# A spectral-convolution kernel: the forward transform along x folded a second time

## The chip, the cores and the metric

The kernel runs on one core of a Trainium2 chip. It is one program with one launch, all in 32-bit floats. The metric is the device time of one execution in microseconds, from the first to the last instruction and what lies around it. The kernel before takes 3254.34 us, the median of three runs (3249.64 to 3259.84).

The core has five instruction queues: TensorE (matrix products, PE in the profile, with its weight loads listed as PEld), VectorE (DVE), ScalarE (ACT), GpSimd (POOL) and SyncE (SP, which here only starts transfers). Each queue is worked off in order; queues wait for each other through semaphores. SBUF is the on-chip memory of 128 partitions, PSUM the small memory into which TensorE writes.

## The reference

The input x has 16 batches, 16 channels and 256 x 256 points. Two layers follow each other, each adding its output to its input.

```python
x = x + L0(group_norm(x))          # a circular 3x3 convolution, 16 -> 16 channels
x = x + L1(group_norm(x))          # a "Laplace" layer:
    alpha = fft2(v)                                        # v: the normalised map
    A, Bm = 1/(i*omega1 - pole1), 1/(i*omega2 - pole2)
    S  = einsum('ikpq,oikp,xikq->oxik', residue, A, Bm)
    x1 = ifft2(einsum('biox,oxik->bkox', alpha, S)).real
    x2 = a few modes: alpha summed against A and Bm, times exponentials in y and x
    return x1 + x2 / 65536
```

So the second layer takes a two-dimensional Fourier transform of 256 maps of 256 x 256, mixes the channels for each pair of frequencies with weights that depend on the frequency, and transforms back. What is changed here is the first of these steps, the forward transform.

## The kernel before, in words

The program has four stages, one after the other.

**Convolution (from 0 to about 764 us).** The convolution of layer 0 is run on TensorE, its output v is written to the scratch tensor `vD` in memory, and the tables that the later stages need are made on the side: `make_hat` fills `tabE`, `tabO` and `hB` from the constants `hatT`, `make_exps` the exponentials. The order of this stage is written out by hand (`manual_schedule`): the loop over `g` issues the convolution's products and advances the table generators by a step now and then.

**Forward transform (about 773 to 1513 us): the stage that is changed.** Its loop runs over the 16 channels `i`, and within each over four groups of four batches `b0`; one such step, of which there are 64, is called a block here. A block has three parts.

- `fold` (lines 583 to 600) loads four maps, `vy`, with the upper and the lower half of y side by side. Since a cosine or sine table of 256 points is symmetric or antisymmetric, the sum and difference of mirrored points can be taken first, and half a table is then enough. GpSimd takes sum and difference of the two halves of y (`s`, lines 590 and 591, 128 x 1024 each). VectorE then folds x in the same way, adding and subtracting the mirrored columns of `s` (`vf`, lines 595, 598 and 599); line 595 also subtracts the mean.
- `lines` (lines 602 to 630) transforms along y: for each of the four maps and each of the two x-parities, one product with `vf` as weights against `tabE` and one against `tabO`, into `ps_y`. Each product of 32-bit floats is two instructions in the profile. ScalarE copies the result to `t` and scales it (line 624).
- `columns` transforms along x: a small product for the few modes of x2 (`psd`, line 637), and for each pair of maps two products of 128 x 128 tables, `sinF` and `cosF`, against 512 columns of `t` (`ps_x`, line 648), one per x-parity. ScalarE copies the odd part to `q` (line 651), VectorE builds the four combinations of even and odd in `spec` (lines 654 to 657), ScalarE and GpSimd set two special frequencies (lines 660 and 661).

After the four blocks of a channel `spec` is written to the scratch tensor `aD` (line 675, started from ScalarE's queue), and `psd` is multiplied with coefficients and summed into `acc` (line 687 on VectorE, line 688 on GpSimd, twice a channel).

The order within this stage isn't written out. The framework's scheduler sets each engine's order from the order of the program, what depends on what, and the number of buffers: three of `vy`, two of `s`, two of `vf`, two of `t`, three PSUM banks for `ps_x`, two of `spec`, one of `pr`.

**Mixing (to about 2440 us)** and **inverse transform (to the end)** follow; in the mixing stage the order is again written by hand. They read `aD` in the order in which the forward transform left the frequencies, and tables (`inv`, `kgrp`) that fit that order. The inverse stage (lines 985 to 1001) ends with sums on VectorE, lines 995 to 1001, beside GpSimd's line 960; these lines are looked at below because they show the two engines at work together.

Of the kernel before, what the change touches and what calls it, by code (L numbers as in the profile page):

```python
# [9 lines left out]
FP = mybir.dt.float32  # L10
AF = mybir.ActivationFunctionType
ALU = mybir.AluOpType
# [5 lines left out]
C = 16  # L18
N = 256
P = 128  # L20
# [4 lines left out]
def conv_then_laplace_kernel(ctx: ExitStack, tc: tile.TileContext, a: dict, out: bass.AP):  # L25
# [15 lines left out]
    nc = tc.nc  # L41
    x = a["x"]
# [4 lines left out]
    def const(name, shape, src=None):  # L47
        t = cp.tile(shape, FP, name=name, tag=name)
        nc.sync.dma_start(out=t, in_=a[name] if src is None else src)
        return t  # L50

    cols = const("cols", [P, 24])
    kmask = const("kmask", [P, C])
    trig = const("trig", [P, 2, P])
    o2 = cp.tile([P, B, 2, 64], FP, name="o2", tag="o2")

    vD = [dp.tile([2, P, C, N], FP, name=f"vD{b}", tag=f"vD{b}") for b in range(B)]
# [22 lines left out]
    tabE = tp.tile([P, C + 1, P], FP, name="tabE", tag="tabE")  # L80
    tabO = tp.tile([P, C + 1, P], FP, name="tabO", tag="tabO")
    hB = tp.tile([P, 2, C, P], FP, name="hB", tag="hB")
    coef = [tp.tile([P, C, 4, 4, 2], FP, name=f"coef{j}", tag=f"coef{j}") for j in range(2)]
    nc.vector.tensor_copy(tabE[:, 0], trig[:, 0])
    nc.vector.tensor_copy(tabO[:, C], trig[:, 1])

# [4 lines left out]
    p1 = ExitStack()  # L93
    wp = p1.enter_context(tc.tile_pool(name="conv_w", bufs=1))
    xp = p1.enter_context(tc.tile_pool(name="xt", bufs=5))
    vp = p1.enter_context(tc.tile_pool(name="vt", bufs=5))
    sp = p1.enter_context(tc.tile_pool(name="stats", bufs=2))
# [14 lines left out]
    def load1(name, shape):  # L112
        t = wp.tile(shape, FP, name=name, tag=name)
        nc.sync.dma_start(out=t, in_=a[name])
        return t
# [2 lines left out]
    imask = load1("imask", [P, 2, 3, 32])  # L118
    g128 = load1("g128", [P, P])
    m16 = load1("m16", [P, C])  # L120
    hatT = load1("hatT", [P, 2, 3, 2, P])
    ones = wp.tile([P, P], FP, name="ones", tag="ones")
    nc.vector.memset(ones, 1.0)

# [184 lines left out]
    def make_hat(side):  # L309


        kcol = sw.tile([P, 2], FP, name="s_kcol", tag="s_kcol")
        nc.sync.dma_start(out=kcol, in_=a["kcol"])
        omega(kcol, kcol, rd[:, side : side + 1])
        n = C * C * 4
        to = ((tabE[:, 1:], tabO[:, :C]), (hB[:, 0], hB[:, 1]))[side]
        for half in range(2):
            pb = sw.tile([P, n // 2, 2], FP, name="s_pb", tag="s_pb")
            nc.sync.dma_start(
                out=pb,  # L320
                in_=a[f"pole{side + 1}"][half * 512 : half * 512 + 512].partition_broadcast(P),
            )
            yield
            re = [sw.tile([P, n // 2], FP, name="s_re", tag=f"s_re{h}") for h in range(2)]
            im = [sw.tile([P, n // 2], FP, name="s_im", tag=f"s_im{h}") for h in range(2)]
            dens = [sw.tile([P, n // 2], FP, name="s_den", tag=f"s_den{h}") for h in range(2)]
            pr, pi = pb[:, :, 0], pb[:, :, 1]
            for h in range(2):
                k = kcol[:, h : h + 1]
                nc.scalar.activation(im[h], pi, AF.Identity, bias=k, scale=-1.0)  # L330
                nc.scalar.activation(dens[h], pi, AF.Square, bias=k, scale=-1.0)
                if h == 0:
                    nc.gpsimd.tensor_tensor(re[1], pr, pr, ALU.mult)
                nc.gpsimd.tensor_tensor(dens[h], dens[h], re[1], ALU.add)
                yield
            for h in range(2):
                w, r, den = im[h], re[h], dens[h]
                nc.vector.reciprocal(den, den)
                yield

                nc.gpsimd.tensor_tensor(r, pr, den, ALU.mult)
                nc.vector.scalar_tensor_tensor(w, w, -1.0, den, ALU.mult, ALU.mult)
                yield
            yield
            for eo in range(2):
                hv = to[eo].rearrange("p i (m r) -> p i m r", r=2)[:, 8 * half : 8 * half + 8]
                for ri in range(2):
                    ps = psu.tile([P, 512], FP, name="ps_setup", tag="ps_setup")
                    for h in range(2):

                        parts = (((2, re), (1, im)), ((0, im), (1, re)))[ri]
                        for j, (at, src) in enumerate(parts):
                            nc.tensor.matmul(
                                ps,
                                lhsT=hatT[:, h, at, eo],
                                rhs=src[h],
                                start=h == 0 and j == 0,
                                stop=h == 1 and j == 1,
                            )
                        yield  # L360
                    nc.scalar.copy(hv[:, :, :, ri], ps.rearrange("p (i m) -> p i m", i=8))
# [173 lines left out]
    for g in range(24 * B + 3):  # L535
        conv(g)
        b, n = divmod(g, 24)
# [22 lines left out]
    p1 = ExitStack()  # L560
    kp = p1.enter_context(tc.tile_pool(name="b_const", bufs=1))
    vp = p1.enter_context(tc.tile_pool(name="vy", bufs=3))
    sp = p1.enter_context(tc.tile_pool(name="fold_y", bufs=2))
    fp = p1.enter_context(tc.tile_pool(name="fold_x", bufs=2))
    lp = p1.enter_context(tc.tile_pool(name="lines", bufs=2))
    kpp = p1.enter_context(tc.tile_pool(name="sines", bufs=3))
# [9 lines left out]
    nc.vector.memset(sgn[:, 0:1], -1.0)  # L576
    nc.vector.memset(sgn[:, 1:2], 1.0)
    acc = kp.tile([P, 2, B, 16, 2], FP, name="acc", tag="acc")
    cosF, sinF = trig[:, 0], trig[:, 1]
    m, n = cols[:, 16:17], cols[:, 17:18]  # L580

    def fold(i, b0):

        vy = vp.tile([P, 2, 4, N], FP, name="vy", tag="vy")
        for j in range(4):
            nc.sync.dma_start(
                out=vy[:, :, j], in_=vD[b0 + j][:, :, i, :].rearrange("h y x -> y h x")
            )
        s = sp.tile([P, 2, 4, N], FP, name="s", tag="s")
        nc.gpsimd.tensor_tensor(s[:, 0], vy[:, 0], vy[:, 1], ALU.add)  # L590
        nc.gpsimd.tensor_tensor(s[:, 1], vy[:, 0], vy[:, 1], ALU.subtract)
        vf = fp.tile([P, 2, 2, 4, P], FP, name="vf", tag="vf")
        lo, hi = s[:, :, :, 0:P], s[:, :, :, N - 1 : P - 1 : -1]
        for j in range(4):
            nc.vector.scalar_tensor_tensor(  # L595
                vf[:, 0, 0, j], lo[:, 0, j], vmr[:, 1, b0 + j, i : i + 1], hi[:, 0, j], ALU.add, ALU.add
            )
        nc.vector.tensor_tensor(vf[:, 0, 1], lo[:, 1], hi[:, 1], ALU.add)  # L598
        nc.vector.tensor_tensor(vf[:, 1], lo, hi, ALU.subtract)
        return vf  # L600

    def lines(i, b0, vf):

# [28 lines left out]
    def columns(i, b0, t, spec, psd):  # L632

        for kq in range(4):
            rows = slice(32 * kq, 32 * kq + 32)
            for xo in range(2):
                nc.tensor.matmul(
                    psd[rows, b0 : b0 + 4],
                    lhsT=hB[:, xo, i, rows],
                    rhs=t[:, xo, :, 1, rows],  # L640
                    start=xo == 0,
                    stop=xo == 1,
                )
        for j in range(0, 4, 2):
            bs = slice(b0 + j, b0 + j + 2)
            ps = [px.tile([P, 2, 2, P], FP, name="ps_x", tag="ps_x") for _ in range(2)]
            for xo, tab in ((1, sinF), (0, cosF)):
                nc.tensor.matmul(ps[xo], lhsT=tab, rhs=t[:, xo, j : j + 2, 0:3:2], start=True, stop=True)  # L648
            even, odd = (z.rearrange("p b t f -> p t f b") for z in ps)
            q = kpp.tile([P, 2, P, 2], FP, name="q", tag="q")  # L650
            nc.scalar.copy(q, odd)
            lo, hi = slice(0, P), slice(P, N)
            st = nc.vector.scalar_tensor_tensor
            st(spec[:, 0, lo, bs], q[:, 1], m, even[:, 0], ALU.mult, ALU.add)
            st(spec[:, 1, lo, bs], q[:, 0], m, even[:, 1], ALU.mult, ALU.subtract)
            st(spec[:, 0, hi, bs], even[:, 0], n, q[:, 1], ALU.mult, ALU.add)
            st(spec[:, 1, hi, bs], even[:, 1], n, q[:, 0], ALU.mult, ALU.subtract)

            flat = spec.rearrange("p r f b -> p (r f) b")
            nc.scalar.copy(flat[:, 0:385:384, bs], even[:, :, 0])  # L660
            nc.gpsimd.tensor_tensor(
                flat[:, 256:127:-128, bs],
                q[:, :, 0],
                sgn.unsqueeze(2).to_broadcast([P, 2, 2]),
                ALU.mult,
            )
# [342 lines left out]
def _constants():  # L1009
# [7 lines left out]
    tcos = np.cos(np.pi * (np.outer(half, p) % (2 * N)) / N)  # L1017
    tsin = np.sin(np.pi * (np.outer(half, f_sin) % (2 * N)) / N)
    c["trig"] = np.stack([tcos, tsin], 1)
    w = 2.0 / N**2  # L1020
    c["inv"] = np.stack([w * tcos.T, w * tsin.T, -w * tsin.T, tcos.T, tsin.T], 1)

    th = 2 * np.pi * (np.outer(j, j) % N) / N
    t = np.stack([np.cos(th), np.sin(th)]).reshape(2, 2, P, N)
    t = np.stack([t[..., :P] + t[..., : P - 1 : -1], t[..., :P] - t[..., : P - 1 : -1]], 3) / 2

    c["hatT"] = np.concatenate([t, -t[:1]]).transpose(2, 1, 0, 3, 4)
    k = (j + P) % N - P
    c["kcol"] = k.reshape(2, P).T
    c["kslot"] = np.concatenate([p, -f_sin])[None]  # L1030
# [14 lines left out]
    cols[:, 20:24] = p[:, None] // 32 == np.arange(4)  # L1045
    c["cols"] = cols

    fx = np.arange(P).reshape(32, 4)
    fx = np.concatenate([fx, [[P, 1, 2, 3]]])
    st = p // 32 % 2  # L1050
    c["kgrp"] = np.where((fx == P) & (st == 0)[:, None, None], -fx, fx)
    mcol = np.zeros((P, 9))
# [89 lines left out]
```

## Time and profile before

| | |
|---|---|
| median of the runs | 3254.34 us |
| the profiled execution | 3263.39 us, span 3261.5 us |
| TensorE busy | 2731.3 us (84% of the span) |
| VectorE busy | 1840.4 us (56%) |
| ScalarE busy | 1342.9 us (41%) |
| GpSimd busy | 942.9 us (29%) |
| mean granted TensorE clock | 0.939 of full speed |
| memory traffic | 193 GB/s over the span |

The profile describes one execution, which took 0.3% more than the median. Its page gives the engines' shares, the queues, the chain of work that ended last and the costliest groups of instructions; the trace behind it can be asked for any stretch: the order of the instructions (the timeline), the busy time by stretch, the duration of every instruction of a line, and who waited for whom. "L595" is line 595 of the kernel before. "128x512" is a tile of 128 partitions with 512 elements in each. In the timeline, consecutive instructions of one line are merged into one entry, with their number behind the x.

### The profile page before, as it was taken

The numbers are of one execution on the slowest core, as the hardware profiler recorded it, in microseconds if no ns is written. First come the engines' busy times: TensorE is split into PE (matmuls) and PEld (weight loads), VectorE is DVE, ScalarE is ACT, GpSimd is POOL, SyncE is SP. The second block draws the span as 40 slices with busy tenths as digits, with TensorE's granted clock in tenths as the row PEclk, the third lists the DMA queues.
The fourth block names the chain that finished last, engine by engine and source line by source line (L and its number), as shares of the span: only waits on it lengthen the run. The fifth ranks groups of instructions, "written<-read, shape, count | busy, mean of one in ns | idle before, by whom it ended". The sixth has DMA issues, their size and how long they took to land.

```text
span 3261.5 us, 104676 instructions
## 1 busy us (share of the span) xinstructions
PE 2731.3 (84%) x46188; PEld 1949.9 (60%) x46188; DVE 1840.4 (56%) x3584; ACT 1342.9 (41%) x2640; POOL 942.9 (29%) x753
## 2 busy tenths in 40 slices
PE   4878787796999999996676777777749999999998
PEld 1333333344777677764444545555438998999987
DVE  5555665565555555555343333334317888788787
ACT  2454676563444444442233333333313333333333
POOL 1111111002444455442111111111105444444442
PEclk9899898898999999997799899999979999999999
DMA  5455565665445555444265555655576776767764
GB/s 215 162 187 172 200 237 195 222 222 171 173 164 203 198 194 185 167 165 182 81 175 160 158 160 163 173 163 168 166 242 231 259 259 235 281 239 252 267 223 155
DMA packets 409158, 637.89 MB, mean 196 GB/s; under 512 B 30336, under 2 KB 364544, under 8 KB 400128
## 3 DMA queue, kind: packets, MB, share of 16 engines
q1 hardware_dynamic: 338816, 496.96, 46.8%
q10 hardware_dynamic: 69888, 134.23, 10.8%
q8 instruction: 364, 5.96, 0.7%
q14 instruction: 90, 0.74, 0.1%
HBM read 353.72 MB, written 277.35 MB: 193 GB/s over the span
## 4 chain that ended last, share of the span: by engine, by line
PE 47%; issue 10%; DVE 4%; DMA 4%; POOL 1%; ACT 1%; ACTq 0%; SPq 0%; DVEq 0%; POOLq 0%
PE ps_s L791 10%; PE ps_mix L839 9%; PE ps_f L990 5%; PE ps_f L991 5%; PE ps_p L985 5%; PE ps_x L648 3%; PE ps_y L608 3%; PE ps_y L616 3%; DMA out_y<-ol 3%; PE ps_h L974 2%; DVE ol L998 1%; DVE ol L1001 1%; DVE ol L997 1%; DVE sg L902 1%; DMA vl<-vD 1%
## 5 line engine op out<-in xcount | busy, mean ns | idle before, releaser
L223 PE MATMUL ps_conv<-xt,wc 32*32 32x512 f32 x12288 | 485.6, 646 | 29.9 <-ACT vt L241 20.8
L960 POOL TENSOR_TENSOR u<-yk 128x512 f32<-128x512 f32 x256 | 340.1, 1357 | 487.9 <-PE ps_p L985 411.3
L791 PE MATMUL ps_s<-ct,w 64*32 64x256 f32 (+1 forms) x8448 | 326.9, 415 | 132.6 <-issue 69.4
L839 PE MATMUL ps_mix<-abd,sg 128*32 128x64 f32 x16384 | 297.7, 229 | 134.9 <-issue 134.5
L839 PEld LDWEIGHTS ps_mix<-abd,sg 128*32 128x32 f32 x16384 | 262.8, 116 | 209.6 <-issue 199.1
L223 PEld LDWEIGHTS ps_conv<-xt,wc 32*32 32x32 f32 x12288 | 230.9, 107 | 235.9 <-issue 144.2
L902 DVE COPY sg<-ps_s 128x512 f32<-128x512 f32 x248 | 172.4, 699 | 342.8 <-PE ps_s L791 342.7
L624 ACT ACTIVATE t<-ps_y,vmr 128x768 f32<-128x768 f32 x256 | 229.7, 900 | 261.0 <-PE ps_y L616 235.9
L767 POOL TENSOR_TENSOR w<-v,mcol 128x2048 f32<-128x2048 f32 x33 | 118.8, 3599 | 717.2 <-DVE v L764 694.1
L608 PE MATMUL ps_y<-tabE,vf 128*128 128x256 f32 x1024 | 308.5, 383 | 17.1 <-DVE vf L595 13.2
L902 ACT COPY sg<-ps_s 128x512 f32<-128x512 f32 x248 | 168.5, 681 | 371.7 <-PE ps_s L791 371.6
L990 PE MATMUL ps_f<-pt,inv 128*128 128x256 f32 x1024 | 318.7, 393 | 0.3
L985 PEld LDWEIGHTS ps_p<-inv,u 128*128 128x128 f32 x2048 | 289.5, 192 | 33.7 <-POOL u L963 14.2
L616 PE MATMUL ps_y<-tabO,vf 128*128 128x256 f32 x1024 | 306.0, 381 | 2.0 <-DVE vf L598 2.0
L791 PEld LDWEIGHTS ps_s<-ct,w 64*32 64x32 f32 x8448 | 163.6, 115 | 239.4 <-issue 113.4
L991 PE MATMUL ps_f<-hs,et 128*128 128x256 f32 x1024 | 305.0, 379 | 0.0
L985 PE MATMUL ps_p<-inv,u 128*128 128x128 f32 x2048 | 291.2, 275 | 13.5 <-POOL u L963 13.5
L993 ACT COPY q<-ps_f 128x256 f32<-128x256 f32 x256 | 95.3, 372 | 432.7 <-PE ps_f L991 388.8
L590 POOL TENSOR_TENSOR s<-vy 128x1024 f32<-128x1024 f32 x64 | 151.7, 2371 | 419.9 <-issue 289.3
L648 PE MATMUL ps_x<-t,trig 128*128 128x512 f32 x512 | 247.3, 605 | 0.0
L253 DVE BATCH_NORM_STATS2 vst<-vt 128x6 f32<-128x512 f32 x128 | 88.0, 687 | 278.1 <-ACT vt L241 278.1
L608 PEld LDWEIGHTS ps_y<-tabE,vf 128*128 128x128 f32 x1024 | 193.9, 191 | 78.9 <-issue 43.8
(197 smaller groups left out, 4162.4 us busy)
## 6 DMA issues: line engine op xcount, KB each, us to landing
xt<-in_x SPq DMA_DIRECT2D x32, 2193.0 KB, 9.4
vD<-vt SPq DMA_DIRECT2D x256, 256.0 KB, 3.1
vy<-vD SPq DMA_DIRECT2D x256, 256.0 KB, 4.2
aD<-spec ACTq DMA_DIRECT2D x16, 4096.0 KB, 14.0
abd<-aD SPq DMA_DIRECT2D x512, 128.0 KB, 3.1
yD<-yt SPq DMA_DIRECT2D x256, 256.0 KB, 4.5
yk<-yD SPq DMA_DIRECT2D x16, 4096.0 KB, 14.2
vl<-vD SPq DMA_DIRECT2D x256, 256.0 KB, 6.3
```

Source lines behind the costliest of these rows:

```text
L223: nc.tensor.matmul(acc[r][32 * c : 32 * c + 32], lhsT=ready[b][0][rows, phase, tap], rhs=halves[b][u // 2][rows, q : q + 5 : 4, 2 - tap : ...
L608: nc.tensor.matmul(ps[:, xo, 0:N], lhsT=vf[:, xo, 0, j], rhs=tabE[:, 0 : i + 2 : i + 1], start=True, stop=False, skip_group_check=True,)
L616: nc.tensor.matmul(ps[:, xo, P : P + N], lhsT=vf[:, xo, 1, j], rhs=tabO[:, i : C + 1 : C - i], start=False, stop=True, skip_group_check=True,)
L624: nc.scalar.activation(t[:, :, j].rearrange("p e l n -> p e (l n)"), ps[:, :, 0:384], AF.Copy, scale=vmr[:, 0, b0 + j, i : i + 1],)
L648: nc.tensor.matmul(ps[xo], lhsT=tab, rhs=t[:, xo, j : j + 2, 0:3:2], start=True, stop=True)
L791: nc.tensor.matmul(ps[odd][32 * iq : 32 * iq + 32, ro, fy], lhsT=w[rows, iq, kk, ro], rhs=ct[rows, iq, kk, fy], start=True, stop=True,)
L839: nc.tensor.matmul(ps[32 * c : 32 * c + 32, j], lhsT=sg[:, 64 * c + 8 * n + j], rhs=abd[n // 2][:, :, c, 8 * (n % 2) + j], start=True, sto ...
L902: (nc.scalar.copy, nc.vector.tensor_copy)[j % 2](o, src)
L960: nc.gpsimd.tensor_tensor(u[:, :, j].rearrange("p b (c n) -> p c b n", c=4), in0, in1, o)
L985: nc.tensor.matmul(ps[:, at], lhsT=u[:, j, n], rhs=tab, start=True, stop=True)
L990: nc.tensor.matmul(ps[:, e], lhsT=tab, rhs=pt[:, e], start=True, stop=False)
L991: nc.tensor.matmul(ps[:, e], lhsT=et[:, 0, k, e], rhs=hs, start=False, stop=True)
```

## The change

The columns of `vf` are folded once more. After the first fold, `vf` holds 128 columns for the even and 128 for the odd x-parity. The change adds and subtracts the mirrored halves of these 128 columns into a new tile `vq`, for the one parity on VectorE and for the other on GpSimd. The products along y take `vq` as weights in place of `vf`, with the same shapes. The transform along x then needs only 64 x 64 tables: in place of two products with 128 x 128 tables for each pair of maps there are four with 64 x 64 tables (`fold2`), each on its own quarter of the TensorE array, with rows 0 to 63 or 64 to 127 of `t` as input and partitions 0 to 63 or 64 to 127 of `ps[xo]` as output.

The frequencies then come out in the order even, odd. The tables that are tied to this order (`inv`, `kgrp`) are permuted on the host; their sizes and uses stay. The x2 table `hB` has to be folded in the same way, so that `hatT` exists in two forms, one for each axis, and is loaded at the beginning of each of the two `make_hat` calls instead of once at the start. The table `trig` is no longer kept in SBUF: its two halves are loaded straight to `tabE[:, 0]` and `tabO[:, C]`, where VectorE copied them before.

The buffers change too: `s` has one instead of two, `vf` one instead of two, and the new `vq` two.

```diff
-    trig = const("trig", [P, 2, P])
...
-    nc.vector.tensor_copy(tabE[:, 0], trig[:, 0])
-    nc.vector.tensor_copy(tabO[:, C], trig[:, 1])
+    nc.sync.dma_start(out=tabE[:, 0], in_=a["trig"][:, 0])
+    nc.sync.dma_start(out=tabO[:, C], in_=a["trig"][:, 1])
...
-    hatT = load1("hatT", [P, 2, 3, 2, P])
...
     def make_hat(side):
+        hatT = wp.tile([P, 2, 3, 2, P], FP, name="hatT", tag="hatT")
+        nc.sync.dma_start(out=hatT, in_=a[f"hatT{side}"])
...
-    sp = p1.enter_context(tc.tile_pool(name="fold_y", bufs=2))
+    sp = p1.enter_context(tc.tile_pool(name="fold_y", bufs=1))
+    f1 = p1.enter_context(tc.tile_pool(name="fold_1", bufs=1))
     fp = p1.enter_context(tc.tile_pool(name="fold_x", bufs=2))
...
-    cosF, sinF = trig[:, 0], trig[:, 1]
+    fold2 = kp.tile([P, 2, 64], FP, name="fold2", tag="fold2")
+    nc.sync.dma_start(out=fold2, in_=a["fold2"])
...
-        vf = fp.tile([P, 2, 2, 4, P], FP, name="vf", tag="vf")
+        vf = f1.tile([P, 2, 2, 4, P], FP, name="vf", tag="vf")
...
-        return vf
+        vq = fp.tile([P, 2, 2, 4, 2, 64], FP, name="vq", tag="vq")
+        for xo, eng in ((0, nc.vector), (1, nc.gpsimd)):
+            lo, hi = vf[:, xo, :, :, 0:64], vf[:, xo, :, :, P - 1 : 63 : -1]
+            eng.tensor_tensor(vq[:, xo, :, :, 0], lo, hi, ALU.add)
+            eng.tensor_tensor(vq[:, xo, :, :, 1], lo, hi, ALU.subtract)
+        return vq.rearrange("p e o b h x -> p e o b (h x)")
...
-            for xo, tab in ((1, sinF), (0, cosF)):
-                nc.tensor.matmul(ps[xo], lhsT=tab, rhs=t[:, xo, j : j + 2, 0:3:2], start=True, stop=True)
+            for h in range(2):
+                rows = slice(64 * h, 64 * h + 64)
+                for xo in range(2):
+                    to = 64 * (h ^ xo)
+                    nc.tensor.matmul(
+                        ps[xo][to : to + 64],
+                        lhsT=fold2[rows, xo],
+                        rhs=t[rows, xo, j : j + 2, 0:3:2],
+                        start=True,
+                        stop=True,
+                    )
...
-    fx = np.arange(P).reshape(32, 4)
-    fx = np.concatenate([fx, [[P, 1, 2, 3]]])
+    fx = o.reshape(32, 4)
+    fx = np.concatenate([fx, [[P, *fx[0, 1:]]]])
```

More of the change, by code (lines that the diff above doesn't have):

```diff
@@ L1019, in _constants @@
     c["trig"] = np.stack([tcos, tsin], 1)
+    o = p.reshape(64, 2).T.ravel()
+    c["fold2"] = np.stack(
+        [
+            np.concatenate([tcos[:64, 0::2], tcos[:64, 1::2]]),
+            np.concatenate([tsin[:64, 1::2], tsin[:64, 0::2]]),
+        ],
+        1,
+    )
     w = 2.0 / N**2
-    c["inv"] = np.stack([w * tcos.T, w * tsin.T, -w * tsin.T, tcos.T, tsin.T], 1)
+    c["inv"] = np.stack([w * tcos.T[o], w * tsin.T[o], -w * tsin.T[o], tcos.T, tsin.T], 1)
     th = 2 * np.pi * (np.outer(j, j) % N) / N
@@ L1025, in _constants @@
     t = np.stack([t[..., :P] + t[..., : P - 1 : -1], t[..., :P] - t[..., : P - 1 : -1]], 3) / 2
-    c["hatT"] = np.concatenate([t, -t[:1]]).transpose(2, 1, 0, 3, 4)
+    t = np.concatenate([t, -t[:1]]).transpose(2, 1, 0, 3, 4)
+    c["hatT0"] = t
+    lo, hi = t[..., :64], t[..., :63:-1]
+    c["hatT1"] = np.concatenate([lo + hi, lo - hi], -1) / 2
     k = (j + P) % N - P
```

## The prediction, made before the result was known

> **What bounds the kernel now.** The change lives in the forward transform, so I first asked for busy times by stretch, then for who waited there, then for the timeline of one block.
>
> The busy times of the stretch from 855 to 1480 us (columns: length; busy us and instructions of PE, PEld, DVE, ACT, POOL; clock, DMA share, GB/s):
>
> ```profile
> 855.00:1480.00 625.00, 622.82 (x3117) 438.19 (x3117) 353.45 (x809) 275.39 (x444) 309.79 (x249) 1.00 0.51 183
> ```
>
> TensorE is busy in 622.82 of 625 us at full clock: it is the bound, and nothing else is near. In the view of waits for 800 to 1480 us, VectorE waits for TensorE (total us, times, longest):
>
> ```profile
> DVE vf L595 <- PE ps_y L616: 255.7, 61, 5.2
> ```
>
> A channel (four blocks) takes 44.93 us in the chain of waits (its start recurs at 1056.64, 1101.55, 1146.49, 1191.44 us), so a block takes 11.23 us. The timeline of one block:
>
> ```profile
> 1306.83 1.88 PE L648 MATMUL ps_x<-t,trig 128*128 128x512 f32 x4
> 1307.03 1.14 DVE L595 SCALAR_TENSOR_TENSOR vf<-s,vmr 128x128 f32<-128x128 f32 x4 [5.12 <-PE ps_y L616]
> 1308.09 0.68 DVE L598 TENSOR_TENSOR vf<-s 128x512 f32<-128x512 f32 x1
> 1308.64 0.66 PE L637 MATMUL psd<-t,hB 128*32 128x128 f32 x16
> 1308.69 1.21 DVE L599 TENSOR_TENSOR vf<-s 128x1024 f32<-128x1024 f32 x1
> 1309.83 0.47 DVE L654 SCALAR_TENSOR_TENSOR spec<-q,cols,ps_x 128x256 f32<-128x256 f32 x1
> 1310.04 2.37 POOL L590 TENSOR_TENSOR s<-vy 128x1024 f32<-128x1024 f32 x1 [6.13 <-issue]
> 1312.37 2.35 POOL L591 TENSOR_TENSOR s<-vy 128x1024 f32<-128x1024 f32 x1
> 1314.69 0.34 POOL L661 TENSOR_TENSOR spec<-q,sgn 128x4 f32<-128x4 f32 x2
> ```
>
> The reader is to see that GpSimd starts `s` 0.2 us after VectorE ends `vf` (its buffer becomes free), so the two never work on SBUF together here. Where they do, it shows at the start of the stage:
>
> ```profile
> 782.51 2.34 POOL L591 TENSOR_TENSOR s<-vy 128x1024 f32<-128x1024 f32 x1
> 782.58 7.37 DVE L595 SCALAR_TENSOR_TENSOR vf<-s,vmr 128x128 f32<-128x128 f32 x4 [3.81 <-POOL s L590]
> 784.80 2.39 POOL L590 TENSOR_TENSOR s<-vy 128x1024 f32<-128x1024 f32 x1
> 787.16 2.39 POOL L591 TENSOR_TENSOR s<-vy 128x1024 f32<-128x1024 f32 x1
> 789.88 0.68 DVE L598 TENSOR_TENSOR vf<-s 128x512 f32<-128x512 f32 x1
> ```
>
> Four VectorE instructions that take 1.14 us elsewhere take 7.37 us, until GpSimd has finished; one gets through at each of its boundaries. The inverse stage says the same of tensor_tensor: L998's row reads "409/419/1500" ns (min, median, max), the long ones beside GpSimd's L960. `spec` (one input in PSUM) keeps its 0.47 us beside GpSimd.
>
> **What the Trainium skill says.** "SBUF — State Buffer", section "Who interferes with whom": a VectorE instruction with two SBUF inputs contends with a GpSimd instruction that reads SBUF, by an exclusive lock held for the whole instruction; with at most one SBUF input it doesn't (outside two-port modes). The trace agrees: 7.37 against 1.14 us, and 0.47 us undisturbed. "TensorEngine Tiling (Array Packing)", "Key Properties": 64x64 gives four tiles that run in parallel, and a change of tiling mode drains TensorE. The trace agrees for smaller tiles: around 1902.87 us, 32 products of 64x256 on 64*32 tiles (L791) take 1.09 us, 0.034 each, where a 256-column product alone takes 0.216. The same page, "Gotcha 1: PSUM Pressure": different row tiles can't use one PSUM bank at once. The change does that (both row halves write `ps[xo]`); no row of the kernel before shows it.
>
> **The change part by part.**
>
> *TensorE.* In the chain of waits two y-products take 0.43 us and four of `ps_x` 1.72. So now: y-products 32 x 0.216 = 6.90 us, `ps_x` 8 x 0.43 = 3.44, `psd` 0.59, gaps and changes of shape 0.20: 11.13. The y-products keep shape and number. The x-products become 16 instructions of 512 columns, eight a pair of maps. Four at a time, a pair takes 2 x 0.43 = 0.86 us; two at a time (the bank rule) 1.72, as now; one at a time 3.44. I take 0.86 plus 0.2 for a drain (the second group now takes 1.91 against 1.72 after `psd`): 2 x 1.06 = 2.1, so a block of about 9.8 us. Bounds: 9.4, 11.3, 14.7.
>
> *VectorE and GpSimd.* Every piece of folding reads two SBUF tiles, so all of it shares one lock, also with GpSimd's other reads. Per block, start to start from the timeline:
>
> - `s` on GpSimd, L590 to L661's start (1310.04 to 1314.69): 4.65
> - L661, two: 0.34
> - L688, 1.27 each, two a channel: 0.63
> - `vf` on VectorE (1307.03 to 1309.83): 2.80
> - sum now: 8.42 of 11.23, so it hides under TensorE
> - added on VectorE: two of 128x512 with two SBUF inputs, like L598, 0.60 start to start: 1.20
> - added on GpSimd: two of 128x512, like L688 (1.27) and L960 (median 1.32): 2.60
> - sum after: 12.22
>
> That is more than TensorE's 9.8 and than today's 11.23. It can't be hidden: the cover (TensorE's time) is gone. The buffers serialise it too: with one `s`, GpSimd can't begin the next `s` before L599 is done; with one `vf`, VectorE can't begin the next before both halves of `vq` are made. The chain s, vf, vq, s is a circle of the same pieces. To the sum I add the channel's end, where L687 waits for L688 (0.80 us now, once in four blocks: 0.20) and hand-overs (0.14 from L599 to L590 now): 12.55 us a block. `spec` (8 x 0.39 = 3.1 us of VectorE, one SBUF input) runs beside GpSimd's 7.3 us of `s` and `vq`; if it stood in the circle, it would add up to 3.1.
>
> Bounds on the block: a VectorE instruction that slips in at a boundary costs GpSimd less than its length (2.34 becomes 2.39 above), which could save some 0.3: 11.9. All of `spec` exposed: 15.7.
>
> *The stage.* The first `s` still ends at 784.85 us. `vf` then needs 2.80, since with one `s` GpSimd no longer runs ahead, and `vq` 3.8: first y-products at about 791.4. The last block ends 63 blocks and its own products (6.9 + 0.6 + 2.1 + 0.3) later: 801.3 + 63 L, with L the block. Now the last x-product ends at 1513.2, so the difference is 63 L - 711.9. For L = 12.55: +79 us. It is zero at L = 11.30.
>
> *The rest.* `fold2` is one more transfer on SP ahead of the `vy` loads (the `jmat` issue took 0.35 us): +0.35. Loading `trig` directly takes away two VectorE copies of 0.23 us at 3.9 us, hidden by the input loads: 0. The second `hatT` load waits on SP for the last product of the first `make_hat`, with stores of `vt` and loads of `xt` behind it. That product is issued two steps of the convolution earlier (the loop has 24 x 16 + 3 = 387 in 760 us, 2 us each), so the wait is 0 to 4 us; `vt` and `xt` have five buffers, and the table is needed eight generator steps (16 convolution steps, some 31 us) later: 0. Permuted tables: 0. The later stages keep their work.
>
> Sum on the profiled execution: 3263.4 + 79 = 3342; on the median, 0.3% lower: 3254 + 79 = 3333 us.
>
> **The rivals.**
>
> *Faster: the lock doesn't set the pace.* If VectorE and GpSimd fold side by side, each alone is below TensorE (VectorE 2.8 + 1.2 + 3.1 + 0.3 = 7.4, GpSimd 4.65 + 0.97 + 2.6 = 8.2), L is 9.8, and 63 x 9.8 - 711.9 = -94: 3160 us. It decides once the shared sum drops below 11.30. For it: no steady block of the kernel before shows the collision. Against: the 7.37 us. Chance 0.08.
>
> *No change: the lock doesn't bind and the tiles don't pack.* Two row halves in one bank leave `ps_x` at 1.72 a pair, L = 11.2 to 11.3, 3250 us. Chance 0.04.
>
> *Slower still: the order wastes the lock.* VectorE is in order; if `spec` stands ahead of `vf` or waits for its PSUM banks, GpSimd waits with it and the lock lies idle. L from 13.3 to 15.7: +126 to +277, 3380 to 3531 us, 3430 in the middle. The same time would come from tiles that run one at a time (L = 14.7). For it: the order is the scheduler's, and L687 already stalls VectorE by 2.7 us a channel. Against: `spec` has 7.3 us of GpSimd work to hide in. Chance 0.23.
>
> *Forecast: the lock's sum, L from 11.9 to 13.3*, +38 to +126. Chance 0.65.
>
> **How the numbers follow.** Predicted 3333, the likeliest. The forecast alone spans 3292 to 3380. For eight in ten the range is 3290 to 3430: the forecast (0.65) and somewhat over half of the slower rival (0.15). Faster or slower than 0.3% (10 us) is about what a measurement can tell from no change: faster 0.08, within 0.04, slower 0.88.
>
> **What would show it.** The stretch's TensorE share falls from 99.7% to about 78%; a channel takes about 50 us instead of 44.93; the y-products wait for `vq`, `vf` waits for GpSimd; L595, L598 or the new VectorE lines have durations far over their 0.35, 0.68 and 0.68 us; GpSimd and VectorE's two-input work add up to nearly the whole block. `ps_x` in timelines: eight in about 1.1 us if the tiles pack, about 1.8 if the bank rule holds. The prediction is wrong if VectorE's two-input lines keep their durations beside GpSimd and TensorE stays at 99%.

## The result, and the profile after

The changed kernel takes 3487.2 us (median; 3480.1 to 3491.7), against 3252.3 us for the kernel before on the same chip: a ratio of 1.072 (1.069 to 1.074), 235 us slower. That is far over the forecast of 3333 us and over the range's upper end of 3430 us. It lies inside the rival "slower still: the order wastes the lock" (3380 to 3531 us). The profiled execution took 3484.5 us, with a span of 3482.7 us.

The last x-product of the forward transform starts at 1742.7 us now and started at 1512.6 us before, so it comes 230 us later. The spans of the two profiled executions differ by 221 us. So the whole loss is in this stage, and the later stages give a little back.

In the changed kernel the lines are shifted: `s` is L594 and L595, `vf` is L599, L602 and L603, `vq` is L608 (sum) and L609 (difference), `t` is L634, `psd` L647, `ps_x` L662, `q` L671, `spec` L674 to L677, its two special frequencies L680 (ScalarE) and L681 (GpSimd), the store of `aD` L695, `pr` L707 and `acc` L708.

The busy times of the stretch from 855 to 1480 us, columns as before (busy us and instructions of PE, PEld, DVE, ACT, POOL; clock, DMA share, GB/s):

```profile
855.00:1480.00 625.00, 494.43 (x2668) 336.15 (x2661) 398.27 (x694) 205.99 (x335) 385.75 (x272) 0.87 0.40 145
```

TensorE's share falls from 99.7% to 79%. That this is so near the 78% that were foreseen is chance: those belonged to a block of 12.55 us, the block is longer than that, and TensorE's work fills 79% of it only because a part of it ran at half clock (the mean granted clock of the stretch is 0.87, where it was 1.00; more on this at the end). Nothing takes TensorE's place: VectorE is busy for 64% of the stretch, GpSimd for 62%. So they take turns, in a circle. The view of waits from 850 to 1650 us (total us, times, longest) says who stands in it:

```profile
ACT spec L680 <- DVE spec L677: 300.1, 106, 8.4
POOL spec L681 <- DVE spec L676: 236.6, 106, 3.1
...
DVE vq L608 <- PE ps_y L626: 166.0, 53, 5.1
...
DVE vf L599 <- POOL vq L609: 108.3, 53, 4.7
...
POOL s L594 <- DVE vf L603: 55.2, 41, 2.5
```

`vf` waits for `vq` and `s` waits for `vf`: that is the circle of buffers that the prediction named. But GpSimd's largest wait is another one: for `spec`. ScalarE's largest wait is for `spec` too: its copy L680 stands in its queue ahead of `t`. The timelines of GpSimd and of VectorE in one block show why (start, length, instruction, and in brackets the idle time before it and what ended it). First GpSimd:

```profile
1311.73 2.34 POOL L594 TENSOR_TENSOR s<-vy 128x1024 f32<-128x1024 f32 x1 [1.31 <-DVE vf L603]
1314.03 2.35 POOL L595 TENSOR_TENSOR s<-vy 128x1024 f32<-128x1024 f32 x1
1316.35 1.71 POOL L608 TENSOR_TENSOR vq<-vf 128x512 f32<-128x512 f32 x1
1318.02 1.71 POOL L609 TENSOR_TENSOR vq<-vf 128x512 f32<-128x512 f32 x1
1322.83 0.20 POOL L681 TENSOR_TENSOR spec<-q,sgn 128x4 f32<-128x4 f32 x1 [3.10 <-DVE spec L676]
...
1325.91 2.35 POOL L594 TENSOR_TENSOR s<-vy 128x1024 f32<-128x1024 f32 x1 [1.31 <-DVE vf L603]
```

Then VectorE:

```profile
1315.39 1.54 DVE L608 TENSOR_TENSOR vq<-vf 128x512 f32<-128x512 f32 x1 [3.80 <-PE ps_y L626]
1316.86 1.75 DVE L609 TENSOR_TENSOR vq<-vf 128x512 f32<-128x512 f32 x1
1319.77 1.14 DVE L599 SCALAR_TENSOR_TENSOR vf<-s,vmr 128x128 f32<-128x128 f32 x4 [1.16 <-POOL vq L609]
1320.82 0.68 DVE L602 TENSOR_TENSOR vf<-s 128x512 f32<-128x512 f32 x1
1321.42 0.48 DVE L674 SCALAR_TENSOR_TENSOR spec<-q,cols,ps_x 128x256 f32<-128x256 f32 x1
...
1324.17 0.48 DVE L677 SCALAR_TENSOR_TENSOR spec<-ps_x,cols,q 128x256 f32<-128x256 f32 x1
1324.56 1.22 DVE L603 TENSOR_TENSOR vf<-s 128x1024 f32<-128x1024 f32 x1
```

The scheduler has put all eight instructions of `spec` between the second and the last part of `vf`. The next `s` needs the last part, so GpSimd stands still meanwhile. The block in order: `s` 4.62 us (1311.73 to 1316.35), `vq` on GpSimd 3.38, hand-over 0.04, the first two parts of `vf` 1.65, `spec` 3.14, L603 1.22, hand-over 0.13: 14.18 us from one `s` to the next. Over a channel it is about 59.5 us, or 14.88 a block, because the channel's end is longer (once in four blocks `pr`, `acc` and the store of `aD` come in). The prediction's own formula gives 63 x 14.88 - 711.9 = +226 us for that; measured were +235.

Two other expectations are read off here. The lock is seen at VectorE's `vq`, which waits for GpSimd (1.54 and 1.75 us in place of 0.68). And the x-products do pack: eight of them, row halves sharing a PSUM bank, take 1.09 us, where four products of 128 x 128 took 1.88:

```profile
1315.29 1.09 PE L662 MATMUL ps_x<-t,fold 64*64 64x512 f32 x8
```

### The profile page after: what moved, and what is told of

It is laid out like the page before. It is cut to its first block, busy times and chain, and to the rows that moved or that the text cites. A ratio compares the mean times of both kernels' runs of the same rounds, so it can differ in the third digit from the quotient of the medians.

```text
span 3482.7 us, 105920 instructions
## 1 busy us (share of the span) xinstructions
PE 2742.6 (79%) x46700; PEld 1943.3 (56%) x46700; DVE 2030.6 (58%) x3710; ACT 1342.1 (39%) x2640; POOL 1174.9 (34%) x881
## 4 chain that ended last, share of the span: by engine, by line
PE 35%; DVE 14%; POOL 14%; issue 8%; DMA 4%; ACT 0%; SPq 0%; ACTq 0%; POOLq 0%; DVEq 0%
PE ps_s L811 9%; PE ps_mix L859 8%; PE ps_f L1010 5%; PE ps_f L1011 4%; PE ps_p L1005 4%; POOL s L595 4%; POOL s L594 4%; DMA out_y<-ol 3%; POOL vq L608 3%; POOL vq L609 3%; PE ps_h L994 2%; DVE vf L599 2%; DVE vf L603 2%; DVE spec L675 1%; DVE spec L676 1%
## 5 line engine op out<-in xcount | busy, mean ns | idle before, releaser
L618 PE MATMUL ps_y<-tabE,vq 128*128 128x256 f32 x1024 | 375.5, 453 | 220.9 <-ACT t L634 204.9
L811 PE MATMUL ps_s<-ct,w 64*32 64x256 f32 (+1 forms) x8448 | 314.5, 402 | 133.4 <-issue 69.8
L618 PEld LDWEIGHTS ps_y<-tabE,vq 128*128 128x128 f32 x1024 | 220.1, 226 | 332.7 <-ACT t L634 229.9
L626 PE MATMUL ps_y<-tabO,vq 128*128 128x256 f32 x1024 | 354.3, 432 | 0.0
L634 ACT ACTIVATE t<-ps_y,vmr 128x768 f32<-128x768 f32 x256 | 231.4, 904 | 204.9 <-PE ps_y L626 198.1
L626 PEld LDWEIGHTS ps_y<-tabO,vq 128*128 128x128 f32 x1024 | 227.6, 222 | 41.7
L239 ACT ACTIVATE vt<-ps_conv,xq 128x512 f32<-128x512 f32 x256 | 161.3, 681 | 177.7 <-PE ps_conv L221 177.4
```

The lines of the kernel that those rows point to most:

```text
L239: nc.scalar.activation(vt if r < 2 else vt[:, ::-1], acc[r], AF.Identity, bias=ready[b][1], **by_sums)
L618: nc.tensor.matmul(ps[:, xo, 0:N], lhsT=vf[:, xo, 0, j], rhs=tabE[:, 0 : i + 2 : i + 1], start=True, stop=False, skip_group_check=True,)
L626: nc.tensor.matmul(ps[:, xo, P : P + N], lhsT=vf[:, xo, 1, j], rhs=tabO[:, i : C + 1 : C - i], start=False, stop=True, skip_group_check=True,)
L634: nc.scalar.activation(t[:, :, j].rearrange("p e l n -> p e (l n)"), ps[:, :, 0:384], AF.Copy, scale=vmr[:, 0, b0 + j, i : i + 1],)
L811: nc.tensor.matmul(ps[odd][32 * iq : 32 * iq + 32, ro, fy], lhsT=w[rows, iq, kk, ro], rhs=ct[rows, iq, kk, fy], start=True, stop=True,)
```

## The experiments

They were made in three groups, each beside the kernel before on its own chip: 3269.1 us for the first four, 3272.6 for the next four, 3256.2 for the last four. Differences are against that.

**1. `spec` behind the folds.** The folds of the next block (all lines of `vf` and `vq`) go ahead of `spec` in VectorE's order. No instruction, buffer or engine changes.

```diff
+        with tc.high_priority():
             lo, hi = s[:, :, :, 0:P], s[:, :, :, N - 1 : P - 1 : -1]
...
```

> The changed kernel with the folding on VectorE (lines of vf and vq) given precedence over spec in each engine's order, so that the two groups of spec no longer stand between the parts of vf; nothing else differs. A block of the changed kernel takes 14.88 us, of which spec takes 3.14 between two parts of vf while GpSimd waits. Theory A (the circle s, vf, vq, s on the shared lock, with spec standing in it): the block falls by about 3.0 to 11.9 us, so 63 x 11.9 - 711.9 = +38 on before, about 3292 us. Rival B (the lock's whole sum, 12.55 us, as forecast): 3333 us. Rival C (the tiled products or TensorE's clock hold the stage up): no change, about 3487 us.

Measured: 3392.6 us, +123 (ratio 1.039, 1.036 to 1.042). So the order alone gives back 111 of the 235 us. That is theory A's direction, but its +38 is missed by far. An ordinary block takes 11.39 us now in place of 14.18 (GpSimd starts `s` at 1201.32, 1212.71 and 1224.10 us). It isn't the forecast's time yet, because the channel's end has become longer: the next two `s` start at 1238.71 and 1253.67 us. ScalarE stands at the store of `aD` there for 2.27 us, with `t` behind it, and a little later for 8.45 us at its copy L681, which waits for `spec`. Its timeline:

```profile
1229.56 1.69 ACT L635 ACTIVATE t<-ps_y,vmr 128x768 f32<-128x768 f32 x2 [2.27 <-POOL spec L682]
...
1240.18 0.16 ACT L681 COPY spec<-ps_x 128x4 f32<-128x4 f32 x1 [8.45 <-DVE spec L678]
```

The copy's wait for `spec` as such isn't new: from 850 to 1650 us it adds up to 275.7 us here and to 300.1 us in the changed kernel. Experiment 6 takes the store away.

**2. The second fold alone.** The folds of the changed kernel stay, and the x-products go back to four of 128 x 128 (a table of blocks, zero elsewhere).

```diff
-            for h in range(2):
...
+            for xo in (1, 0):
+                nc.tensor.matmul(
+                    ps[xo], lhsT=fold2[:, xo], rhs=t[:, xo, j : j + 2, 0:3:2], start=True, stop=True
+                )
```

> The changed kernel with its second fold, its buffers and its order of frequencies, but the x-products as before: two products a pair with 128 x 128 tables, whose quarters are the 64 x 64 tables or zero. TensorE's block is back at about 11.1 us. Theory A (the folding sets the pace): as slow as the changed kernel, about 3487 us, within 20, because TensorE's longer block is hidden. Rival C (the tiled products, their shared PSUM banks or the changes of tiling mode cost the time): it comes down towards the lock's sum, 3333 us or less.

Measured: 3492.4 us, +223 (1.069, 1.067 to 1.070): the changed kernel's time, though TensorE works some 1.5 us longer in each block (1.88 and 1.98 us for its two groups of x-products in place of 1.09 and 1.27). The whole loss comes with the fold, its buffers and its order, and the gain in TensorE's work is hidden behind it.

**3. The tiles alone.** The x-products on four 64 x 64 tiles, and no second fold; `s` and `vf` have two buffers again.

```diff
-    sp = p1.enter_context(tc.tile_pool(name="fold_y", bufs=1))
+    sp = p1.enter_context(tc.tile_pool(name="fold_y", bufs=2))
...
-        vf = f1.tile([P, 2, 2, 4, P], FP, name="vf", tag="vf")
+        vf = fp.tile([P, 2, 2, 4, P], FP, name="vf", tag="vf")
...
-        vq = fp.tile([P, 2, 2, 4, 2, 64], FP, name="vq", tag="vq")
...
-        return vq.rearrange("p e o b h x -> p e o b (h x)")
+        return vf
```

> The changed kernel without its second fold: vf goes to the y-products as before (two buffers of s and of vf, no vq), only the x-products are the four 64 x 64 tiles; it leaves out the second fold, so its numbers are not the transform's. Theory A (the tiled products work as meant and the fold costs the time): TensorE is the bound with a block of 9.8 us, 63 x 9.8 - 711.9 = -94, about 3160 us. Rival C (tiles sharing a PSUM bank don't overlap, or the changes of mode eat the gain): 3250 us or more.

Measured: 3243.0 us, -26 (0.993, 0.990 to 0.995), where -94 was expected. The sign is right and the size isn't. Most blocks take 9.97 us (`psd` starts at 1199.15, 1209.06, 1218.97 and 1228.94 us), but the one at the channel's end takes 14.38 (the next `psd` starts at 1243.32); of the 15 channel ends 12 are like this one, and the others take 11.6 to 12.7 us. ScalarE's and TensorE's timelines there:

```profile
1237.32 0.33 ACTq L689 DMA_DIRECT2D aD<-spec  x1
1237.70 1.69 ACT L628 ACTIVATE t<-ps_y,vmr 128x768 f32<-128x768 f32 x2 [2.83 <-POOL spec L675]
...
1238.65 1.21 PE L612 MATMUL ps_y<-tabE,vf 128*128 128x256 f32 x2 [2.46 <-ACT t L628]
```

ScalarE starts the store of `aD` (L689) only when GpSimd has finished the channel's last L675, at 1237.29 us, for one `acc` sum stands ahead of that in GpSimd's queue. `t` (L628) stands behind the store, PSUM isn't emptied, and TensorE waits for 2.46 us. It then runs the next products at half speed for 3.6 us (more on this at the end).

**4. All of `vq` on VectorE.** This takes the slower copy of the fold off GpSimd and leaves the order.

```diff
-        for xo, eng in ((0, nc.vector), (1, nc.gpsimd)):
+        for xo, eng in ((0, nc.vector), (1, nc.vector)):
```

> The changed kernel with all four instructions of the second fold on VectorE, none on GpSimd. GpSimd's part of the lock falls by 2.6 us a block and VectorE's rises by 1.2: the sum falls from 12.22 to 10.8. VectorE's own work rises to 8.7 us. Theory A (the circle): spec still stands between the parts of vf and two more VectorE instructions wait for GpSimd's boundaries, so the block is about 12.5 us, +76, about 3330 us. Rival B (the lock's sum alone): 11.2 us with hand-overs and the channel's end, about 3248 us. Rival D (VectorE's total work is the bound, not the lock): slower than the changed kernel, over 3487 us.

Measured: 3387.1 us, +118 (1.035, 1.033 to 1.038). That is 117 us less than the change as it was made: VectorE takes 0.60 us where GpSimd took 1.25 or more. It is slower than the +76 expected. One reason is that the lock stretches `vq` where it meets the next `s`; how much of the missing 42 us this explains was not worked out. VectorE's timeline:

```profile
1247.33 1.76 DVE L608 TENSOR_TENSOR vq<-vf 128x512 f32<-128x512 f32 x1 [1.27 <-PE ps_y L626]
1249.01 2.84 DVE L609 TENSOR_TENSOR vq<-vf 128x512 f32<-128x512 f32 x1
```

**5. The tiles alone, the store in SyncE's queue.** Experiment 3 with its new wait taken away: the store of `aD` is started from SyncE's queue.

```diff
-        nc.scalar.dma_start(
+        nc.sync.dma_start(
```

> The kernel of pack_only (tiled x-products, no second fold, so again not the transform's numbers) with one edit: the store of spec to aD, once a channel, is issued from SP's queue instead of ScalarE's. In pack_only three blocks of a channel take 9.97 us and the fourth 14.3, 44.17 us a channel; there ScalarE's queue stands still at the store until GpSimd's L675, which is queued behind s and L702, and the evictions to t wait behind it. Theory E (that wait in ScalarE's queue makes the channel's end): the fourth block falls to about 10.5, the stage by 16 x 3.8 = 60 us, to about 87 us under before. Rival F (the channel's end comes from L701 and L702 on VectorE and GpSimd, not from the store): as pack_only, 26 us under before.

Measured: 3198.6 us, -74 (0.977, 0.975 to 0.979), where theory E gave -87. The 48 us between this and experiment 3 were ScalarE's queue; some 19 of them (12 ends, 1.6 us each) came through the half clock that follows the wait. `psd` now recurs every 9.97 us, with 10.31 once a channel (1201.67, 1211.64, 1221.95, 1231.91, 1241.88 us).

**6. `spec` behind the folds, the store in SyncE's queue.** Experiment 1 with the same one-word edit.

> vf_first with the same single edit, the store of spec on SP's queue. In vf_first a block takes 11.39 us away from the channel's end but 13.09 on average. Theory E: the average falls to about 11.9 and the time from 123 us over before to about 45 over. Rival G (the channel's end is long because GpSimd does L709 twice between s and vq, on the circle, and the order slips for two blocks): 100 us over before or more. In no theory does it get faster than before, since 11.39 alone is above 11.30.

Measured: 3343.7 us, +71 (1.021, 1.019 to 1.023), where the prediction gave +79 for the changed kernel; theory E's +45 for this run is missed, and theory G's 100 too. This is the order that the prediction had in mind: the folds share the lock, and `spec` runs beside GpSimd. GpSimd's timeline of one block:

```profile
1232.26 2.37 POOL L594 TENSOR_TENSOR s<-vy 128x1024 f32<-128x1024 f32 x1 [3.05 <-issue]
1234.59 2.36 POOL L595 TENSOR_TENSOR s<-vy 128x1024 f32<-128x1024 f32 x1
1236.90 1.25 POOL L682 TENSOR_TENSOR spec<-q,sgn 128x4 f32<-128x4 f32 x2
1238.11 1.27 POOL L609 TENSOR_TENSOR vq<-vf 128x512 f32<-128x512 f32 x1
1239.34 1.27 POOL L610 TENSOR_TENSOR vq<-vf 128x512 f32<-128x512 f32 x1
1243.65 2.37 POOL L594 TENSOR_TENSOR s<-vy 128x1024 f32<-128x1024 f32 x1 [3.04 <-issue]
```

and VectorE's beside it:

```profile
1236.79 0.71 DVE L609 TENSOR_TENSOR vq<-vf 128x512 f32<-128x512 f32 x1 [1.52 <-PE ps_y L627]
...
1240.64 1.14 DVE L600 SCALAR_TENSOR_TENSOR vf<-s,vmr 128x128 f32<-128x128 f32 x4 [2.54 <-POOL vq L610]
```

`s` 4.64, VectorE's `vq` 1.21 (GpSimd's L682 waits through it), GpSimd's `vq` 2.50, `vf` 2.88, hand-overs 0.16: 11.39 us. The prediction's terms for the same pieces are 4.65, 1.20, 2.60, 2.80 and 0.14: 11.39. Its 0.34 us for L661 (now L682) are not among them, since L682 lies beside VectorE's `vq`. The channel's end adds 3.2 us (the block that starts its `vf` at 1203.24 us lasts to 1217.87, 14.63 us), 0.81 a block, where the prediction had 0.63 and 0.20. With a block of 12.20 us the prediction's formula gives +57; the other 14 us aren't in that sum. In most channels the first block after the end is longer as well (up to 12.85 us from one `s` to the next), and the stage's first block takes 27.0 us from one `psd` to the next, where the kernel before takes 13.0.

**7. Two buffers of `s`.** The changed kernel with a second buffer of `s`, which was to free `s` from the circle (`vy` with two buffers, three before, to make room).

```diff
-    vp = p1.enter_context(tc.tile_pool(name="vy", bufs=3))
-    sp = p1.enter_context(tc.tile_pool(name="fold_y", bufs=1))
+    vp = p1.enter_context(tc.tile_pool(name="vy", bufs=2))
+    sp = p1.enter_context(tc.tile_pool(name="fold_y", bufs=2))
```

> The changed kernel with two buffers of s instead of one, and two of vy instead of three to make room; the order of the engines' work is left to the scheduler. Theory A (the circle through the single s, with spec inside): GpSimd need not wait for the last part of vf; but GpSimd's L681 waits for spec and stands ahead of the next s in its order, so only the 1.3 us from L681 to the end of L603 are saved, part of which L603 takes back by waiting for the lock: a block of about 14.2 us, some 190 us over before. Rival H (the cut in buffers is the cause): within 60 us of before.

Measured: 3501.2 us, +229 (1.069, 1.067 to 1.072), the time of the changed kernel, and 39 us more than theory A gave. GpSimd still waits for `spec`, because L681 stands in its queue ahead of the next `s`; waits from 850 to 1650 us:

```profile
POOL spec L681 <- DVE spec L676: 239.7, 107, 3.1
...
POOL s L594 <- DVE vf L603: 54.9, 41, 2.5
```

With its second buffer GpSimd runs one block further ahead and then waits for L603 as before (55.2 us in the changed kernel). The single buffer of `s` is therefore not what makes the change slow; the order closes the circle a second time. Two buffers of `vf`, which has one in place of two as well, were not tried.

**8. Less work on GpSimd.** Experiment 1, and the sum of `s` and all of `vq` on VectorE as well, so that GpSimd keeps one instruction of 128x1024 a block.

```diff
-        nc.gpsimd.tensor_tensor(s[:, 0], vy[:, 0], vy[:, 1], ALU.add)
+        nc.vector.tensor_tensor(s[:, 0], vy[:, 0], vy[:, 1], ALU.add)
```

> An attempt at a faster kernel with the whole change: the sum half of s (L594) and all of the second fold on VectorE, GpSimd keeps only the difference half of s, L682 and L709; vf and vq have precedence over spec as in vf_first. The lock's sum falls to 1.14 + 2.33 + 0.97 + 2.80 + 2.40 = 9.6 us, VectorE's work rises to 1.14 + 2.8 + 2.4 + 3.1 + 0.34 = 9.8. Theory A (the lock and the circles on it set the pace): a block of 10.3 to 11.0 us away from the channel's end and 11.0 to 11.8 with it, 20 us under to 35 over before. Rival D (VectorE, in order and nearly full, becomes the bound with its waits): 80 us over before or more.

Measured: 3322.5 us, +50 (1.015, 1.013 to 1.017), between the numbers of the two theories. Two blocks of a channel take 9.94 us, then come two long ones of 12.7 and about 15.4, at the channel's end. VectorE's timeline and ScalarE's show where:

```profile
1238.60 0.69 DVE L708 TENSOR_TENSOR pr<-psd,coef 128x512 f32<-128x512 f32 x1 [1.16 <-POOL acc L709]
...
1248.55 0.16 ACT L681 COPY spec<-ps_x 128x4 f32<-128x4 f32 x1 [9.66 <-DVE spec L678]
```

`pr` waits for the `acc` sum before it, and stands ahead of `vq` on VectorE; then `spec` comes late, and ScalarE waits 9.66 us for it with `t` behind.

**9 to 11. The same with the channel's end freed.** The store in SyncE's queue and two buffers of `pr` (`sines`, three before, with two); then `pr` ahead in VectorE's order too (the last lines of the diff, in the second of the three only); or two buffers of `s`.

```diff
-    prp = p1.enter_context(tc.tile_pool(name="prod", bufs=1))
+    prp = p1.enter_context(tc.tile_pool(name="prod", bufs=2))
...
+                with tc.high_priority():
                     nc.vector.tensor_tensor(pr, psd, cf, ALU.mult)
```

> The kernel less_on_pool (folds ahead on VectorE, the sum of s and all of vq on VectorE, 1 product of s left on GpSimd) with the channel's end freed as well: the store of aD in SyncE's queue, two buffers of pr (and two of the sines, three before). Nothing is left out. Theory I (what less_on_pool lost on its short blocks of 9.94 us stood at the channel's end: ScalarE's queue behind the store, pr behind the accumulation): the average block goes from 12.1 to between 10.3 and 11.0 us, 63 x (10.3 to 11.0) - 712 = 63 to 19 us under the time before, ratio 0.98 to 0.994. Theory J (VectorE's own order: spec behind the folds, and ScalarE's copy behind spec): the wait stays whoever stores; the average block stays at 11.6 or more, at least 20 us over the time before, ratio 1.006 or more.

> less_on_pool_ends with L708 (pr) put ahead in VectorE's order too. Theory I: as less_on_pool_ends within 15 us, since pr has its second buffer already. Theory J: 20 us or more under it, because psd's single buffer comes free with pr and t waits for psd.

> less_on_pool_ends with two buffers of s (and two of vy, three before). Theory I or J alone: within 15 us of less_on_pool_ends, since with 2.4 us of GpSimd's work a block s is no longer what a block waits for. If the single buffer of s still closes the circle (s, vf, s), it is 25 us or more under it.

Measured: 3232.9 us (0.994, 0.992 to 0.996), 3223.3 us (0.988, 0.984 to 0.992) and 3239.4 us (0.994, 0.992 to 0.996). All three are faster than the kernel before, by 0.6 to 1.2%. Theory I holds, at the slow edge of what it gave: what experiment 8 lost stood at the channel's end. `pr` ahead is worth 10 us more at the middle, within theory I's 15, but the intervals touch, so that its own share isn't settled (the last section has more on this); a second `s` is worth nothing. In the second of them TensorE and VectorE are both near the end of what they have (stretch from 855 to 1480 us):

```profile
855.00:1480.00 625.00, 593.88 (x3808) 409.40 (x3801) 593.89 (x1136) 289.83 (x475) 236.12 (x204) 1.00 0.53 192
```

This is the best version with the second fold in it: 33 us under the kernel before, where the change as it was made is 235 us over.

**12. The control: the store's place in the kernel before.**

> The control: the kernel before with only its store of aD moved from ScalarE's queue to SyncE's. If the 48 us between pack_only and pack_store_sp came from the store holding ScalarE in a kernel whose TensorE has slack, the kernel before, where TensorE is the bound, moves by no more than 10 us (ratio 0.997 to 1.0). If the store's place is worth its 48 us whatever the kernel, ratio 0.985.

Measured: 3252.0 us (0.998, 0.997 to 1.000), 4 us less. The store's place costs next to nothing where a block lasts 11.23 us, and 48 us where it lasts 9.97.

## Why the prediction was wrong, point by point

- **The direction and the mechanism were right.** The folds share the lock, the circle of `s`, `vf`, `vq` sets the pace, and TensorE's gain is hidden. Experiment 2 shows the last: TensorE's longer work changes nothing. What the runs don't separate is the lock from the buffers: with one `s` and one `vf`, most pieces of the circle would follow each other without a shared port too. In the block of experiment 6 the lock itself is seen only at L682, whose two instructions take 1.25 us in place of 0.34.
- **The step that failed:** "`spec` (8 x 0.39 = 3.1 us of VectorE, one SBUF input) runs beside GpSimd's 7.3 us of `s` and `vq`". It could, but it didn't: in VectorE's order it stands before the last part of `vf`, and GpSimd waits for it, once for the buffer of `s` and once for L681. The measured 3.14 us stand in the circle. The prediction had this as a bound (15.7 us for a block) and as a rival with a chance of 0.23, and argued against it that `spec` has work to hide in. That work doesn't help when an in-order queue puts `spec` first; the order of the kernel before, `vf` in one piece and then `spec`, was taken over without a reason, although each of the new waits could move it.
- **The sum of the other terms holds.** With `spec` behind the folds and the store moved (experiment 6), an ordinary block takes 11.39 us, which is what the same terms gave, and the kernel is slower by 71 us where 79 were predicted. That the two are so close is luck in part: the 0.34 us of L661 aren't paid (21 us over 63 blocks), and 14 us come in that the formula doesn't have. From the forecast of 12.55 to the 14.88 measured in the changed kernel: +3.14 for `spec`; -0.34 for L661 (now L681), whose length lies inside the wait for `spec`; -0.42 because VectorE's `vq` slips in between GpSimd's instructions (3.38 us for both engines' `vq` in place of 1.20 + 2.60); +0.07 for `s`, `vf` and the hand-overs; -0.13 at the channel's end (0.70 in place of 0.83). Sum: 14.87.
- **TensorE's block was right:** 9.8 us predicted, 9.97 measured in experiments 3 and 5. The rival "the tiles don't pack" falls with the 1.09 us for eight products.
- **The rival "faster" was mispriced.** Its -94 us took a block of 9.8 us from end to end. With no second fold at all, and so no new use of the lock, the kernel gains 26 us only, because the channel's end holds TensorE through ScalarE's queue, and 74 us with the store moved. A wait of a few us once a channel was free under TensorE's 11.23 us and is not under 9.97.
- **The things costed at nothing** (tables, `hatT`, `fold2`) were not tried one by one. Experiments 3 and 5 contain them all and are faster than before, so they hide no large cost.

The Trainium skill, "SBUF — State Buffer", "Who interferes with whom", says that the shared ports are held for a whole instruction and that the order of issue decides who is blocked. Experiment 6 agrees on both: GpSimd's L682, 0.35 us elsewhere, takes 1.25 us behind VectorE's `vq`, and in the changed kernel VectorE's `vq` takes 1.54 and 1.75 us behind GpSimd's `s` and `vq`. "TensorEngine Tiling (Array Packing)", "Gotcha 1: PSUM Pressure", says that different row tiles can't use one PSUM bank at a time. The 1.09 us for eight products, two row halves to a bank, do not agree; the measurement decides.

## What to carry to other kernels

When work moves from the engine that is the bound to engines that share a resource, first draw the circle that the buffers close and then ask where each engine's in-order queue will put the work that is *not* in it: three microseconds of `spec` that could hide cost 111 us because the order put them inside. When the bound gets shorter, the waits at the ends of the outer loop that it used to cover come out, here a store in the queue of an engine that must empty PSUM, worth 4 us in the kernel before and 48 us in experiment 3. And with two engines on one lock, giving most of the work to the faster one was better here than sharing it (+50 us in experiment 8, +123 in experiment 1).

## What the runs showed of the hardware that was not expected

After a wait TensorE can run at half its clock for 3.4 us. In experiment 3 it waits for 2.46 us (1236.19 to 1238.65 us), and the next y-products take 0.85 us a pair in place of 0.43. A wait of 2.47 us in the channel before (1193.69 to 1196.16 us) isn't followed by this. The traces show why. All 2044 changes of the clock in the fourteen profiles lie on a grid of 3.413 us, whatever TensorE does at that moment; so the clock is set anew once in each window of this length, and what counts is how long TensorE stands idle within one window. Three windows of experiment 3 (the length comes first, then TensorE's busy time; the granted clock is the third value from the end):

```profile
1194.33:1197.74 3.41, 1.58 (x7) 1.42 (x8) 0.69 (x1) 1.69 (x2) 1.74 (x3) 1.00 1.09 391
1235.29:1238.70 3.41, 0.95 (x6) 0.49 (x4) 0.69 (x1) 1.00 (x2) 2.77 (x5) 1.00 0.59 204
1238.70:1242.11 3.41, 3.41 (x8) 2.46 (x8) 0.00 (x0) 0.69 (x1) 0.50 (x1) 0.50 1.01 427
```

The first wait lies across an edge of the grid: 1.83 us of it fall into the window from 1194.33 us on, and the clock stays full. The second lies within one window, 2.46 us, and the window after it has half the clock. Of the 4.4 us by which this channel's last block is longer, 2.46 are the wait and some 1.9 the clock (3.61 us for four groups of two, 1.73 at full clock).

The same count over the forward stages of all fourteen profiles, from 830 us on, gives 2755 windows at full clock. After 212 of them the clock is halved; in all but two of these (1.80 and 1.97 us) TensorE is idle for 2.0 us or more. After the others it stays full, and none of these is idle for more than 2.01 us. Of 286 windows at half clock 213 are followed by full clock, each with at most 0.58 us idle, and 73 by half clock again, each with at least 0.60 us idle. The profile models the ends of the products, so that these limits are approximate. The Trainium skill, "TensorE: Matmul & The Clock Gate", "What's actually happening", ties the half clock to an idle window of some 3.4 us that runs freely; the grid agrees, while here 2.0 us of idle time in one window were enough.

In the changed kernel the half clock isn't what costs the time: from 850 to 1650 us GpSimd waits for y-products for 2.1 us in all, and experiment 2, with a mean clock of 0.94 in the stretch where the changed kernel has 0.87, is as slow. In experiment 9 half clock follows 10 of the channel ends, and in experiment 10, with `pr` ahead, none. From the first to the last x-product their stages take 693.2 and 676.8 us, and 10 times 1.6 us are nearly all of this difference.
